# Rotary attention on one NeuronCore: which step of eight holds which small piece of work

## The chip, the cores and the metric

The kernel runs on one core of a Trainium2 chip. It is one program that computes a whole stack of eight blocks for 2048 tokens of width 256. The metric is the device time of one execution in microseconds; of the kernel before there are three timed runs and one profiled execution. Five engines work side by side: PE (TensorE, matmuls and transposes; its weight loads are listed apart as PEld), DVE (VectorE), ACT (ScalarE), POOL (GpSimd) and SP, which here only issues DMAs. Each engine takes its instructions in a fixed order and waits where one of them is not ready.

## The reference, cut to what matters

The change lies in the seventh block, an attention with rotary positions. The tokens are 32 sequences of 64 with 256 features, but the block sees each sequence as 64 channels over 256 positions; its context has the same shape. There are 8 heads of 8 channels:

```
N_HEADS, CHANNELS = 8, 64
K_CH = CHANNELS // N_HEADS
q = split_heads(_proj(x, Wq, bq))
k = split_heads(_proj(c, Wk, bk))
v = split_heads(_proj(c, Wv, bv))
q = _apply_rotary(q_emb, q)
k = _apply_rotary(k_emb, k)
scores = jnp.einsum('bhtc,bhsc->bhts', q, k) / math.sqrt(K_CH)
p_attn = jax.nn.softmax(scores, axis=-1)
out = jnp.einsum('bhts,bhsc->bhtc', p_attn, v)
out = out.transpose(0, 1, 3, 2).reshape(b, N_HEADS * K_CH, t_t)
return _proj(out, Wo, bo)
...
x = x + jnp.tanh(g_xattn[3]) * _L3_xattn_ref(_layernorm(x, axis=-1), ctx_2048, ...)
```

So each of the 32 sequences has 8 score matrices of 256 x 256, a softmax over their rows, a product with the values and an output projection.

## The kernel before, in words

The whole stack is one program. Blocks 4 and 5 run as one software pipeline; the rotary block (block6, line 1590) begins inside the end of that pipeline and then runs alone; the last block, a feed-forward with a Walsh-Hadamard transform (block7, line 1873), follows, and prepares its weights (weights7, line 1850) and its first statistics during the rotary block.

block6 is a hand-written schedule of steps, numbered g. From line 2038 on, PE, DVE, ACT and POOL keep the order in which the program names their instructions. Sequence s has two passes of four steps each:

- Steps 4s to 4s+3, the pass for the maxima. In each, `scores` (line 1675) makes a quarter of the score matrices (pp, line 1700), and DVE takes the row maxima straight from PSUM (line 1710).
- Steps 4s+6 to 4s+9, the pass for the weights. In each, `scores` makes a quarter of the transposed scores (pw, line 1686), adds the negated maxima with one more product per head (sel by top, line 1693), and ACT takes the exponential from PSUM (e, line 1706).

So from step 6 to step 127 each step first issues, for two different sequences, pw with its sel products, then pp, then the exponential and the maximum. pw and pp are 32-row matmuls that use different row strips of the array. Their PSUM tiles are a pair of banks each, taken in turn from three buffers (`pair`, line 1609), in the order pw, pp, pw, pp. A buffer is free again when ACT has taken the exponential of its pw, or DVE the maximum of its pp. So the pp of a step takes the buffer of the pw of the step before, and the pw of a step takes the buffer of the pp of two steps before.

After that each step runs the small pieces whose `due` names it (lines 1752 to 1824), in the order in which they were registered. All pieces that use PE share a pool of two PSUM banks (c.aux). They are, for sequence s, or for the pair i of sequences 2i and 2i+1:

- split (line 1662), step 4s+3: DVE, two small reductions that turn the maxima into two parts.
- shift (line 1667), step 4s+5: PE transposes the maxima twice 128 x 128 (L1671), ACT copies them to top (L1673). The sel products of step 4s+6 are the first to need them.
- mix (line 1712), steps 4s+8 and 4s+10: PE multiplies the exponentials with the values, 8 products of 128 rows by 32 columns, recorded as 16 matmuls (L1717), ACT copies the result to po_sb (L1720).
- normalise (line 1722), steps 8i+13 and 8i+15 for the two sequences: PE transposes four times (pn, L1728), DVE takes a reciprocal and a product (L1730, L1732).
- turn (line 1734), step 8i+17: two transposes (pot, L1737), ACT copies to oT (L1739).
- finish (line 1741), step 8i+23: the output projection (py, L1743), ACT adds the bias and applies the gate (y, L1745), POOL adds to x (L1746).

By the step's number modulo 8, the pieces on PE are then: 0 mix; 1 turn, then shift; 2 mix; 3 none; 4 mix; 5 normalise, then shift; 6 mix; 7 finish, then normalise.

Every 16 steps the queries of two more pairs of sequences and their keys are made (lines 1760 to 1802): in step 3 of the sixteen the query projection (`_queries`, line 402: L413 on PE, L416 on ACT, L417 on DVE), in steps 8 and 10 the queries and keys are split into two parts each (`_split_slowly`, line 464: POOL L466, then ACT L468, then POOL L470), in steps 9 and 11 DMAs on SP spread them over the partitions. These pieces are registered before the others, so in their step they come first. weights7 puts four matmuls into step 11 of some sixteens (L1859), and POOL work into later ones.

Of the kernel before, what the change touches and what calls it, by code (L numbers as in the profile page):

```python
# [1589 lines left out]
def block6(c):  # L1590
# [11 lines left out]
    with ExitStack() as es:  # L1602
# [151 lines left out]
        def due(step, what, *args):  # L1754
            steps[step].append((what, args))

        def of(what, s, *args):
            return lambda: what(seqs[s], *args)
# [47 lines left out]
        for i in range(B // 2):  # L1806
            last = i == B // 2 - 1
            for s in (2 * i, 2 * i + 1):
                due(4 * s + 3, of(split, s))
                due(4 * s + 5, of(shift, s))  # L1810
                due(4 * s + 8, of(mix, s, 0))
                due(4 * s + 10, of(mix, s, 1))
            due(8 * i + 13, of(normalise, 2 * i))
            due(8 * i + 15, of(normalise, 2 * i + 1))
            due(8 * i + 17, of(turn, 2 * i + 1))
            due(8 * i + (19 if last else 23), of(finish, 2 * i + 1))

        due(8, lambda: bias())
# [107 lines left out]
def program(tc, a, out):  # L1926
    nc = tc.nc
    with ExitStack() as es:
# [109 lines left out]
        with tc.manual_schedule(engines={mybir.EngineType.PE, mybir.EngineType.DVE, mybir.EngineType.Activation, mybir.EngineType.Pool}):  # L2038

            sixth, g, made, before6 = None, 0, 0, prologue6(c, c.first6)  # L2040
            for k, (past, done4) in enumerate(pipe):
                if past == 0 and k % 4 == 0 and made < 10 or past == 1 and k % 10 == 0:
                    next(before6, None)
                    made += 1
                if done4:
                    if sixth is None:
                        for _ in before6:
                            pass
                        k4.close()
                        keep.close()  # L2050
                        c.third = None
                        sixth = block6(c)
                        next(sixth)
                    elif k % 6 == 0:
                        next(sixth)
                        g += 1
# [131 lines left out]
```

## Time and profile before

| | us |
|---|---|
| median of three runs (lowest, highest) | 1277.58 (1267.42, 1283.98) |
| profiled execution, its own time | 1276.41 |
| its span, first to last instruction | 1274.6 |
| rotary block, steps 16 to 127 | 868.0 to 1088.6 |
| PE, DVE, ACT busy in these 220.6 us | 198.16, 174.06, 163.09 |
| mean granted TensorE clock, whole span | 0.954 |

How to read the profile: times count from the span's start. A timeline line gives the start, the duration, the engine, the line in the kernel, the operation, the tiles written and read, their shapes, how many instructions were merged, and in brackets how long the engine had been idle before and what ended that. `pw<-top,sel` is written pw, read top and sel. A line of waits gives who waited, for whom, the total time, how often and the longest. A step can be found in the timeline by the first weight load of its pw (PEld L1686), since each step begins with four of them. "issue" means that nothing the profile shows ended the wait.

### The profile page before, as it was taken

What the parts mean: (1) busy time and instruction counts of PE and PEld (TensorE: products, weight loads), DVE (VectorE), ACT (ScalarE), POOL (GpSimd) and SP (SyncE); (2) the same over time, 40 slices, a digit from 0 to 9 for tenths busy, and PEclk for the clock granted to TensorE, in tenths of its full rate; (3) what the DMA queues carried; (4) which work ended last, traced back from release to release, by engine and by line L of the source; (5) the groups of instructions that cost most, each with busy time, mean ns of one, the idle gap of its engine ahead of it and who ended that gap; (6) DMA issues with size and microseconds to landing.
All of it is one profiled execution on the core that took longest, in us unless ns stands there. A gap on an engine that the chain in (4) does not pass through costs nothing.

```text
span 1274.6 us, 21379 instructions
## 1 busy us (share of the span) xinstructions
PE 1141.2 (90%) x8086; PEld 697.0 (55%) x8086; DVE 856.8 (67%) x2133; ACT 654.0 (51%) x1131; POOL 461.7 (36%) x544
## 2 busy tenths in 40 slices
PE   3797899999999999998789998678999988999998
PEld 2575644545453337776566665335555545465565
DVE  5476858653644989877799999867878777522111
ACT  3556464331213114555789998457777767511110
POOL 3226150503012324333477777944444454000000
PEclk9988999999999999998999999759999889999999
DMA  6221010010014214000000000215334322000000
GB/s 230 96 75 66 17 42 9 1 67 1 0 74 159 67 34 170 1 1 1 2 2 2 2 2 2 67 42 182 90 94 105 98 56 53 1 14 5 16 17 17
DMA packets 26776, 62.99 MB, mean 49 GB/s; under 512 B 4144, under 2 KB 9008, under 8 KB 25520
## 3 DMA queue, kind: packets, MB, share of 16 engines
q1 hardware_dynamic: 26384, 61.60, 15.3%
q8 instruction: 64, 1.05, 0.3%
q14 instruction: 40, 0.33, 0.1%
q10 hardware_dynamic: 288, 0.00, 0.0%
HBM read 37.48 MB, written 8.39 MB: 36 GB/s over the span
## 4 chain that ended last, share of the span: by engine, by line
PE 48%; DVE 26%; POOL 8%; issue 8%; ACT 6%; DMA 2%; SPq 1%; POOLq 0%; ACTq 0%; DVEq 0%
PE pc L755 5%; PE po L1921 4%; PE pu L1911 4%; PE pg L1911 4%; PE po L1717 2%; PE pu L610 2%; PE pu L607 2%; PE pg L607 2%; PE pg L610 2%; ACT e L1706 2%; DVE xn L169 2%; PE pa L654 2%; PE po L660 1%; DVE e L1291 1%; PE pw L1686 1%
## 5 line engine op out<-in xcount | busy, mean ns | idle before, releaser
L1710 DVE TENSOR_REDUCE mx<-pp 128x4 f32<-128x1024 f32 x128 | 155.7, 1218 | 47.1 <-PE pp L1700 28.4
L1706 ACT ACTIVATE e<-pw 128x1024 f32<-128x1024 f32 x128 | 130.4, 1024 | 50.5 <-PE pp L1700 26.6
L613 ACT ACTIVATE sg<-pg 128x512 f32<-128x512 f32 (+1 forms) x75 | 37.8, 511 | 104.7 <-PE pg L607 55.9
L755 PE MATMUL pc<-xw,wb 64*64 64x512 f32 x768 | 90.0, 600 | 0.2 <-DVE x L687 0.2
L1913 ACT ACTIVATE sg<-pg 128x512 f32<-128x512 f32 x32 | 19.1, 597 | 122.8 <-PE pg L1911 122.7
L614 DVE TENSOR_TENSOR h<-pu,sg 128x512 f32<-128x512 f32 (+1 forms) x75 | 42.8, 575 | 54.5 <-PE pu L607 34.4
L1717 PE MATMUL po<-e,va 128*32 128x256 f32 x1024 | 75.1, 415 | 4.5 <-DVE t L417 2.9
L1914 DVE TENSOR_TENSOR h<-pu,sg 128x512 f32<-128x512 f32 x32 | 22.1, 691 | 80.7 <-PE pu L1911 80.4
L1700 PE MATMUL pp<-x,x 32*128 32x256 f32 x512 | 69.3, 354 | 4.3 <-ACT e L1706 4.0
L1686 PE MATMUL pw<-x,x 32*128 32x256 f32 x512 | 66.7, 344 | 2.6 <-DVE mx L1710 1.5
L1693 PE MATMUL pw<-top,sel 32*128 32x512 f32 x256 | 56.1, 441 | 10.1 <-ACT top L1673 8.4
L1686 PEld LDWEIGHTS pw<-x,x 32*128 32x128 f32 x512 | 40.4, 197 | 44.1 <-issue 26.4
L913 POOL TENSOR_TENSOR acc<-acc,sq 128x512 f32<-128x512 f32 x28 | 39.0, 1392 | 65.0 <-ACT sq L912 63.6
L1911 PE MATMUL pu<-xf,wa 128*128 128x512 f32 x128 | 60.3, 593 | 0.0
L1911 PE MATMUL pg<-xf,wa 128*128 128x512 f32 x128 | 60.3, 593 | 0.0
L755 PEld LDWEIGHTS pc<-xw,wb 64*64 64x64 f32 x768 | 30.0, 134 | 53.2 <-issue 52.5
L1921 PE MATMUL po<-hb,h 128*128 128x256 f32 x256 | 55.9, 379 | 0.0
L1921 PEld LDWEIGHTS po<-hb,h 128*128 128x128 f32 x256 | 48.8, 191 | 8.2 <-issue 1.9
L112 DVE BATCH_NORM_STATS2 ln_st<-x 128x6 f32<-128x256 f32 x112 | 44.4, 408 | 11.5 <-POOL x L1746 6.7
L1488 PE MATMUL pm<-w,xqT 128*128 128x512 bf16 x128 | 40.7, 424 | 11.0 <-DVE sh L1137 8.0
L1700 PEld LDWEIGHTS pp<-x,x 32*128 32x128 f32 x512 | 41.4, 202 | 9.3 <-ACT e L1706 6.3
L610 PE MATMUL pu<-zu,wa 128*128 128x512 f32 (+1 forms) x100 | 43.2, 526 | 3.4 <-DVE h L614 3.4
(361 smaller groups left out, 2981.8 us busy)
## 6 DMA issues: line engine op xcount, KB each, us to landing
x<-t SPq DMA_DIRECT2D x64, 128.0 KB, 2.6
x<-kt SPq DMA_DIRECT2D x56, 128.0 KB, 2.7
w<-in_l2f SPq DMA_DIRECT2D x12, 512.0 KB, 3.9
keys<-k_t SPq DMA_DIRECT2D x8, 512.0 KB, 3.4
wa<-in_l0f SPq DMA_DIRECT2D x2, 1828.0 KB, 11.5
kt<-keys SPq DMA_DIRECT2D x7, 512.0 KB, 3.5
wa<-in_l1f SPq DMA_DIRECT2D x2, 1536.0 KB, 8.6
wa<-in_l3f SPq DMA_DIRECT2D x6, 512.0 KB, 7.2
```

Source lines behind the costliest of these rows:

```text
L112: ins = c.nc.vector.bn_stats(st, c.x[:, i, :])
L607: nc.tensor.matmul(p, wt[:, k, fc], xf[:, k, :N], start=k == 0, stop=False, skip_group_check=True)
L610: nc.tensor.matmul(p, wt[:, fc], z[m, s][:, :N], start=False, stop=s == 1, skip_group_check=True)
L755: nc.tensor.matmul(pcs[h][to], w[rows, k, m, h, :], xw[rows, k, h, :, Z - m : Z - m + 32], start=m == 0, stop=m == Z)
L1686: nc.tensor.matmul(pw[:, jj, k, :], w.k[rows, h, k * P : (k + 1) * P], w.q[rows, h, :], start=k == 0, stop=False, skip_group_check=True,)
L1693: nc.tensor.matmul(pw[:, jj], sel[rows, h, :], top, start=False, stop=True, skip_group_check=True)
L1700: nc.tensor.matmul(pp[:, jj, n, :], p.q[rows, n, t * P : (t + 1) * P], p.k[rows, n, :], start=n == 0, stop=True, skip_group_check=True,)
L1706: nc.scalar.activation(e, pw, AF.Exp, scale=scale)
L1710: nc.vector.tensor_reduce(p.mx[:, t, i0 : i0 + 2, 4:6], pp, AX.X, ALU.max)
L1717: nc.tensor.matmul(po[strip(j), :], vas[a.i % 3][:, a.n, k, 2 * j + h, :], a.e[h, j][:, k, :], start=k == 0, stop=k == 1)
L1911: nc.tensor.matmul(p, wt[:, k, fc], xf[:, k, :], start=k == 0, stop=k == 1)
L1921: nc.tensor.matmul(po, h[:, f, q * P : (q + 1) * P], c.w2h[:, f, :], start=f == 0, stop=f == NH - 1)
```

## The change

The change moves small pieces between steps; no instruction is added, removed or altered.

- shift goes from step 4s+5 to step 4s+4, that is from steps 1 and 5 of eight to steps 0 and 4, where it comes behind the mix of the sequence before.
- normalise goes from 8i+13 to 8i+14 for the first sequence of a pair (step 6 of eight, behind the mix there) and from 8i+15 to 8i+18 for the second (step 2 of eight, ahead of the mix there, because it is registered earlier).
- turn goes from 8i+17 to 8i+21 (step 5 of eight). finish stays at 8i+23.
- For the last pair of sequences, the steps of the second normalise and of turn are 8i+16 and 8i+18.

By the step's number modulo 8 the pieces on PE are afterwards: 0 mix, then shift; 1 none; 2 normalise, then mix; 3 none; 4 mix, then shift; 5 turn; 6 mix, then normalise; 7 finish.

```diff
@@ -1807,12 +1807,12 @@
             last = i == B // 2 - 1
             for s in (2 * i, 2 * i + 1):
                 due(4 * s + 3, of(split, s))
-                due(4 * s + 5, of(shift, s))
                 due(4 * s + 8, of(mix, s, 0))
+                due(4 * s + 4, of(shift, s))
                 due(4 * s + 10, of(mix, s, 1))
-            due(8 * i + 13, of(normalise, 2 * i))
-            due(8 * i + 15, of(normalise, 2 * i + 1))
-            due(8 * i + 17, of(turn, 2 * i + 1))
+            due(8 * i + 14, of(normalise, 2 * i))
+            due(8 * i + (16 if last else 18), of(normalise, 2 * i + 1))
+            due(8 * i + (18 if last else 21), of(turn, 2 * i + 1))
             due(8 * i + (19 if last else 23), of(finish, 2 * i + 1))
```

## The prediction

> **What bounds the kernel now.** First the page's busy times, then the waits, then the stretch that the change touches, in order of time.
>
> ```profile
> span 1274.6 us, 21379 instructions
> PE 1141.2 (90%) x8086; PEld 697.0 (55%) x8086; DVE 856.8 (67%) x2133; ACT 654.0 (51%) x1131; POOL 461.7 (36%) x544
> ```
>
> PE is the engine to fill, but 90% is a mean. The rotary block's steps 16 to 127 run from 868.0 to 1088.6 us; there PE is busy for 198.16 of 220.60 us. The waits of this stretch (who waited, for whom; total, times, longest) say what ends PE's idle time:
>
> ```profile
> PEld pw L1693 <- ACT top L1673: 15.1, 27, 0.8
> PE pw L1693 <- ACT top L1673: 7.7, 14, 0.6
> PE pt L1671 <- ACT po_sb L1720: 5.9, 6, 2.1
> PE pp L1700 <- ACT e L1706: 3.7, 5, 0.9
> ```
>
> The first three belong to shift, which the change moves. The fourth is the one to remember: the maxima's product (pp) waits until an exponential has emptied a buffer. I then read the timeline of steps 112 to 119, which hold no other work: 14.1 us, steps beginning with the weight loads of pw at 1060.41, 1062.08, 1063.35, 1065.90, 1066.37, 1069.18, 1070.65, 1072.74 and 1074.48.
>
> ```profile
> 1062.08 0.30 PEld L1686 LDWEIGHTS pw<-x,x 32*128 32x128 f32 x4 [0.41 <-issue]
> ...
> 1063.35 0.30 PEld L1686 LDWEIGHTS pw<-x,x 32*128 32x128 f32 x4 [0.17 <-issue]
> ...
> 1064.46 0.18 PEld L1693 LDWEIGHTS pw<-top,sel 32*128 32x128 f32 x2 [0.82 <-ACT top L1673]
> ...
> 1065.90 0.30 PEld L1686 LDWEIGHTS pw<-x,x 32*128 32x128 f32 x4 [0.41 <-issue]
> ...
> 1066.37 0.31 PEld L1686 LDWEIGHTS pw<-x,x 32*128 32x128 f32 x4
> ...
> 1066.67 1.94 ACT L1706 ACTIVATE e<-pw 128x1024 f32<-128x1024 f32 x2 [0.26 <-PE pp L1700]
> ...
> 1067.75 0.30 PEld L1700 LDWEIGHTS pp<-x,x 32*128 32x128 f32 x4 [0.95 <-ACT e L1706]
> ...
> 1068.18 0.59 PEld L1717 LDWEIGHTS po<-e,va 128*32 128x32 f32 x16
> 1069.18 0.19 PEld L1686 LDWEIGHTS pw<-x,x 32*128 32x128 f32 x2 [0.41 <-issue]
> ```
>
> The step at 1065.90 has no extra work on PE, and lasts 0.47 us. The next pays for it: with three pair buffers, pp must wait for the exponential of the empty step, so the mix starts at 1068.18, **2.28 us after the empty step began** (0.77 to the exponential, 0.97 for it, 0.11 to pp, 0.43 to the mix). So a pair "odd step, next even step" never lasts less than 2.28 us plus the even step's extra work, however empty the odd one is. The pair's two products take 0.68 of an even step before its extra work (1062.08 to 1062.76 in the step with turn and shift), so an odd step hides the latency only if it lasts 2.28 - 0.68 = 1.60 us or more.
>
> In every second eight (steps 8 to 10 of 16) a query conversion sits on ACT:
>
> ```profile
> 949.39 0.62 ACT L468 CAST t<-t 128x512 fp32r<-128x512 f32 x1 [0.73 <-POOL t L466]
> 949.92 0.36 ACT L1720 COPY po_sb<-po 128x256 f32<-128x256 f32 x1
> 950.18 1.03 ACT L1706 ACTIVATE e<-pw 128x1024 f32<-128x1024 f32 x1
> 950.33 0.20 PEld L1671 LDWEIGHTS pt<-ident,mx 128*128 128x128 f32 x2 [0.99 <-ACT po_sb L1720]
> ```
>
> And the granted clock (the column before the last two) halves for a while in some such eights; the first row is an eight at full clock, the second the worst:
>
> ```profile
> 946.80:961.90 15.10, 13.63 (x165) 8.48 (x164) 12.63 (x27) 12.08 (x21) 6.09 (x6) 1.00 0.53 128
> 1006.70:1027.40 20.70, 19.35 (x165) 10.97 (x164) 13.53 (x27) 12.52 (x21) 6.07 (x6) 0.67 0.51 127
> ```
>
> **The change part by part.** Nothing is added or removed; shift (2 transposes, ACT copy to top) moves from odd steps into the mix steps 0 and 4 of eight, normalise (4 transposes, DVE reciprocal and product) into mix steps 6 and 2, turn from step 1 to 5. None of them issues a DMA or a POOL instruction, and finish with its POOL addition stays, so the queues of SP and POOL keep their order. Afterwards steps 1 and 3 are empty, 5 holds two transposes, 7 one product.
>
> Prices, by differences of steps in the timeline. The mix: 1069.18 - 1068.18 = 1.00. Shift alone on PE: pt's load at 950.33 to the next pw at 950.70, 0.37; I take 0.36. Normalise: its four loads begin at 1073.73 and the next pw at 1074.48, 0.75 later; 0.17 of that is the gap ahead of pw, which a mix step pays anyhow (its own is 0.41): 0.58. After a mix, eight transposes at 1094.05 take 1.15 to the next pw, 0.14 each, so both prices hold behind a mix too.
>
> Eight clean steps, by pairs (before from the starts above; after is 2.28 plus the even step's work):
> - 1 and 2: 3.82 (with the wait for top) becomes 2.28 + 1.00 + 0.58 = 3.86: +0.04. The wait for top goes, the wait for the exponential comes in its place.
> - 3 and 4: 3.28 becomes 2.28 + 1.00 + 0.36 = 3.64: +0.36. Step 3 was empty before too, so shift is paid in full.
> - 5 and 6: 3.56 becomes 2.28 + 1.58 = 3.86: +0.30.
> - 7 and 0: 1.74 + 1.67 = 3.41 becomes 2.28 + 1.36 = 3.64: +0.23. Step 7 loses normalise, falls from 1.74 to some 1.2 and no longer covers its exponential; step 5, with turn alone, to 1.0.
> Sum +0.93 on 14.1 us; two such eights at the end: +1.9.
>
> Sixteen steps with queries and conversions (six of them, steps 16 to 111): the pairs as above, +0.04, +0.36 (in step 3 DVE's query instructions set when the mix may start, in both kernels; shift comes on top), +0.30, then steps 7 to 10 together, +0.36, +0.30, +0.23. For 7 to 10: the cast starts 4.3 us after step 7 in both, since POOL's work before it is the same. Before, PE then waits for the copy of po and again for top: steps 7 to 10 last 1.74 + 1.67 + 2.23 + 2.53 = 8.17. Afterwards ACT does cast, copy of po, copy of top, exponential of step 9; pp of step 10 is queued on PE behind that exponential, and the mix, normalise and all later steps behind pp. Exponential from 5.4 to 6.4 after step 7, pp at 6.5, extras at 6.95, plus 1.58: 8.55, so +0.4. Sum +2.0 per sixteen, six times: +11.9.
>
> Costed at nothing: shift's wait for split, which DVE ends by 1068.4 where shift would begin at 1069.2 (behind the queries, 0.4 us early still; if late, that lateness is added to the pair). DVE's product and reciprocal, 0.54 us, only change their step; DVE is busy 11.18 of the 14.1 us of the eight. The two small PSUM buffers: in the new order (po pt, pn po, po pt, pot, po pn, py) each is taken again at least a step after its reader was issued. The first 16 steps are led by the blocks before (PE waits up to 6.2 us for their DVE there): 0, between -2 and +2. The last steps, where pp is gone: 0, between -1 and +1.
>
> Two costs have no row. Array shapes: in the new even steps 32-row, 128*32 and 128*128 matmuls follow one another. The load behind a mix waits 0.41 on "issue", behind transposes 0.17, behind pp 0.25. Least: transposes cost 0.11 each (shift in step 5: 1.47 - 1.25 = 0.22 for two): 56 even steps at -0.14 are -8. Most: 0.41 more in each: +23. I take 0, since the eight transposes behind the mix show none.
>
> The Trainium skill, TensorEngine Tiling (Array Packing), Key Properties, says that changing the tiling mode drains TensorE. By that rule it counts against the change: I count 16 switches in eight steps for 14 before, and with 0.41 for each added one 2 x 14 x 0.41 = 11.5 us would come on top.
>
> Clock: the drops at 888.6, 919.3, 1011.5 and 1049.0 us cost 1.2, 3.1, 5.6 and 1.5, 11.4 in all, by their eights against 15.1 (less 1.3 of an ACT wait in the last). Each follows steps 9 and 10, where PE idles 0.75 + 0.59 = 1.34 us. Afterwards step 10 idles about 1.35: the same, so 0. Ends: all drops gone, -11; one like the worst in each of the six, 33.6 - 11.4 = +22.
>
> The Trainium skill, TensorE: Matmul & The Clock Gate, Why this matters for your kernels, asks only for no idle gap over about 3 us; by it no drop would come at all and the sum would be 11 us lower. The trace differs: its drops follow idle pieces under 1 us.
>
> **Sum** against the profiled execution's 1276.4 (span 1274.6 and 1.8 around it): 11.9 + 1.9 = +13.8, so 1290.2. The median shown is 1277.6, 1.2 above: 1291.
>
> **The rivals.**
> - *Nothing takes the place of the waits removed* (other side): PE's idle time for top and po_sb, 7.7 + 5.9 = 13.6, is won: 1264. For it: these are the largest waits of PE here. Against: 1065.90 to 1068.18. It decides if the even step's work can begin earlier than 2.28 us after an odd step's start; the break-even is 2.28 - 0.93 / 4 = 2.05.
> - *The clock becomes the bound*: +8 to +22 on the forecast, 1299 to 1313. For it: more steps idle 0.6 us, and step 10's idle time lies closer together. Against: no clean eight shows a drop.
> - *Changes of shape cost 0.41 in each even step*: 1291 + 23 = 1314. Against: the eight transposes behind a mix.
>
> **How the numbers follow.** Forecast 0.60, own range 1282 to 1300 (shape prices at -8, the ends of the stretch at +3, and about half the 16.6 us between the runs shown); waits won 0.12; clock 0.16; shapes 0.12. Two per cent, about what a measurement of this kernel can tell from no change, is below 1252 or above 1303. Slower: half the clock case and two thirds of shapes, 0.16; faster: 0.02; same: 0.82. Leaving out about 0.08 below and 0.11 above, the range is 1270 to 1308.
>
> **What would show it.** Right: pw no longer waits for top except in step 10 of 16; pp's wait for e grows from 5 to some 50 times, about 0.6 us each; pairs of 3.86 and 3.64; a clean eight of about 15.0. Wrong: pairs under 3.5 (the latency is hidden), mix steps longer by over 0.36 and 0.58 than a bare mix (shapes), or half clock over more than 27 us of the stretch.

## The result, and the profile after

The changed kernel takes 1287.35 us (median of 17 runs, 1282.77 to 1290.75); the kernel before, over 17 runs beside them, 1273.7. The ratio is 1.0109, with a 95% interval from 1.0086 to 1.0133: slower by about 14 us, where the forecast was +13.8. The profiled execution, the slowest of the 17 runs, has a span of 1289.0 us, 14.4 more than before.

The page's first lines:

```profile
span 1289.0 us, 21362 instructions
...
PE 1152.0 (89%) x8070; PEld 694.5 (54%) x8086; DVE 859.4 (67%) x2133; ACT 655.9 (51%) x1131; POOL 462.3 (36%) x544
```

The program's instructions are the same (a few PE records are missing from the trace). PE is nevertheless busy 10.8 us longer. In the clean eight from step 112 it is busy 13.34 of 15.1 us, for 12.70 of 14.1, although its matmuls, added up one by one, take 56.5 us for 56.9: fewer of them run side by side. So a higher busy time of PE is no sign of more work here, and of the 1.0 us by which the eight grew only 0.4 show as idle time of PE. The waits of the rotary block after the change (who, for whom; total, times, longest):

```profile
PEld pp L1700 <- ACT e L1706: 25.1, 33, 1.2
...
PE pp L1700 <- ACT e L1706: 13.3, 19, 0.9
...
PEld pw L1693 <- ACT top L1673: 8.3, 6, 2.7
...
PE pw L1693 <- ACT top L1673: 7.1, 6, 2.5
```

The wait for top is left in six places only, one for each conversion, where it became longer (7.1 us in 6 waits of PE, for 7.7 in 14). pp's wait for the exponential has taken the place of the others, from 3.7 to 13.3 us. The timeline of steps 112 to 114, which begin at 1071.81, 1074.17 and 1074.42:

```profile
1072.80 0.59 PEld L1717 LDWEIGHTS po<-e,va 128*32 128x32 f32 x16
...
1073.80 0.20 PEld L1671 LDWEIGHTS pt<-ident,mx 128*128 128x128 f32 x2 [0.41 <-ACT e L1706]
...
1074.17 0.18 PEld L1686 LDWEIGHTS pw<-x,x 32*128 32x128 f32 x2 [0.17 <-issue]
...
1074.42 0.30 PEld L1686 LDWEIGHTS pw<-x,x 32*128 32x128 f32 x4
...
1074.95 1.94 ACT L1706 ACTIVATE e<-pw 128x1024 f32<-128x1024 f32 x2 [0.29 <-PE pw L1693]
...
1076.03 0.30 PEld L1700 LDWEIGHTS pp<-x,x 32*128 32x128 f32 x4 [1.13 <-ACT e L1706]
...
1076.46 0.42 PEld L1728 LDWEIGHTS pn<-ident,po_sb 128*128 128x128 f32 x4
...
1077.04 0.59 PEld L1717 LDWEIGHTS po<-e,va 128*32 128x32 f32 x16 [0.17 <-issue]
...
1078.05 0.18 PEld L1686 LDWEIGHTS pw<-x,x 32*128 32x128 f32 x2 [0.41 <-DVE rl L1730]
```

The empty step at 1074.17 is left after 0.25 us, the next one's pw is issued at once, and then PE waits: the even step's own work (pn) begins at 1076.46, 2.29 us after the empty step did. The same stretch also shows the two prices: mix to pt 1.00, pt to the next pw 0.37; pn to the mix 0.58.

| pair of steps (clean eight) | before | forecast | after |
|---|---|---|---|
| 1 and 2 | 3.83 | 3.86 | 3.87 |
| 3 and 4 | 3.28 | 3.64 | 3.65 |
| 5 and 6 | 3.56 | 3.86 | 3.87 |
| 7 and 0 | 3.40 | 3.64 | 3.65 |
| eight | 14.1 | 15.0 | 15.05 |

Where the span's 14.4 us lie, by the starts of steps: up to step 16, 865.9 for 868.0, -2.1; the six sixteens with conversions (steps 16 to 111) 205.9 for 192.4, +13.5; the two clean eights 30.11 for 28.15, +2.0; from step 128 on 187.06 for 186.03, +1.0.

### The profile page after: what moved, and what is told of

Read it like the earlier page. It is cut to its first block, busy times and chain, and to the rows that moved or that the text cites. A ratio compares the mean times of both kernels' runs of the same rounds, so it can differ in the third digit from the quotient of the medians.

```text
span 1289.0 us, 21362 instructions
## 1 busy us (share of the span) xinstructions
PE 1152.0 (89%) x8070; PEld 694.5 (54%) x8086; DVE 859.4 (67%) x2133; ACT 655.9 (51%) x1131; POOL 462.3 (36%) x544
## 4 chain that ended last, share of the span: by engine, by line
PE 53%; DVE 25%; POOL 7%; issue 6%; ACT 6%; DMA 1%; SPq 0%; POOLq 0%; ACTq 0%; DVEq 0%
PE pc L755 5%; PE po L1921 4%; PE pu L1911 4%; PE pg L1911 4%; PE po L1717 4%; ACT e L1706 2%; PE pu L610 2%; PE pu L607 2%; PE pg L607 2%; PE pg L610 2%; PE pw L1686 2%; PE pa L654 2%; DVE xn L169 2%; PE po L660 1%; PE pp L1700 1%
## 5 line engine op out<-in xcount | busy, mean ns | idle before, releaser
L1700 PE MATMUL pp<-x,x 32*128 32x256 f32 x512 | 69.3, 354 | 15.0 <-ACT e L1706 13.3
L1686 PE MATMUL pw<-x,x 32*128 32x256 f32 x512 | 63.2, 340 | 3.1 <-DVE mx L1710 1.7
L1693 PE MATMUL pw<-top,sel 32*128 32x512 f32 x256 | 51.9, 420 | 7.1 <-ACT top L1673 7.1
L1700 PEld LDWEIGHTS pp<-x,x 32*128 32x128 f32 x512 | 41.5, 202 | 29.8 <-ACT e L1706 25.1
L1746 POOL TENSOR_TENSOR x<-x,y 128x256 f32<-128x256 f32 x16 | 11.8, 735 | 109.5 <-ACT y L1745 96.4
L1488 PE MATMUL pm<-w,xqT 128*128 128x512 bf16 x112 | 38.8, 422 | 13.1 <-DVE sh L1137 7.9
```

What stands on the lines that cost most here:

```text
L1686: nc.tensor.matmul(pw[:, jj, k, :], w.k[rows, h, k * P : (k + 1) * P], w.q[rows, h, :], start=k == 0, stop=False, skip_group_check=True,)
L1693: nc.tensor.matmul(pw[:, jj], sel[rows, h, :], top, start=False, stop=True, skip_group_check=True)
L1700: nc.tensor.matmul(pp[:, jj, n, :], p.q[rows, n, t * P : (t + 1) * P], p.k[rows, n, :], start=n == 0, stop=True, skip_group_check=True,)
```

## The experiments

The theory: a pair of an odd and the next even step lasts the longer of two things, PE's work in it, or the 2.28 us from the odd step's start over its exponential and pp to the even step's extra work, plus that work. Rivals: array shapes changing in the mix steps; the waits that the change took away; the clock. All ratios are to the kernel before, run on the same chip; lengths of steps come from one profiled execution of each kernel.

**Shift alone.** Only shift goes to step 4s+4.

```diff
-                due(4 * s + 5, of(shift, s))
                 due(4 * s + 8, of(mix, s, 0))
+                due(4 * s + 4, of(shift, s))
```

> Only shift moves (to steps 0 and 4 of eight); normalise and turn stay in odd steps. Latency theory (a pair of an odd and the next even step lasts 2.28 us plus the even step's extra work, or the sum of the PE work if that is longer): pairs 1+2 3.28, 3+4 3.64, 5+6 3.28, 7+0 3.78, so a clean eight (steps 112 to 119) of 13.98 us against 14.1 before and 15.06 in the changed kernel; whole kernel within 3 us of the kernel before. Rival, changes of the array's shape in the mix steps cost the time: 28 of the 56 moved pieces stand behind a mix here too, so half of the changed kernel's loss, about +7 us, and pairs 3+4 and 7+0 longer than 3.64 and 3.78.

Measured: pairs 3.29, 3.65, 3.29 and 3.76, the eight 14.0 us: the steps are as the latency theory has them, and no half of the loss is here. The sixteen from step 48, at full clock in both, lasts 29.5 us for 29.8. The time is not as expected: 1278.59 us, ratio 1.0042 (1.0007 to 1.0077), some 5 us slower, outside the 3 us expected. In its profiled execution one eight took 20.0 us, at two thirds of the clock (third number from the end):

```profile
881.90:901.90 20.00, 18.45 (x162) 9.90 (x160) 11.62 (x17) 12.20 (x20) 6.09 (x6) 0.66 0.53 133
```

The kernel before has such an eight as well, of 20.70 us. And this execution is the fastest of the ten (1272.63 us); its steps 16 to 127 take 217.6 us, for 220.5 in the profile of the kernel before, so the loss of the median can't be read from it. The ten runs had mean clocks of 0.932 to 0.950, those of the kernel before 0.944 to 0.960. That left the clock as a suspect, which later runs test.

**Normalise and turn alone.** Shift stays in 4s+5; the other lines are as in the change.

```diff
-            due(8 * i + 13, of(normalise, 2 * i))
-            due(8 * i + 15, of(normalise, 2 * i + 1))
-            due(8 * i + 17, of(turn, 2 * i + 1))
+            due(8 * i + 14, of(normalise, 2 * i))
+            due(8 * i + (16 if last else 18), of(normalise, 2 * i + 1))
+            due(8 * i + (18 if last else 21), of(turn, 2 * i + 1))
```

> Only normalise and turn move; shift stays in steps 1 and 5. Latency theory: the wait for top stays and the odd steps get emptier: pairs 1+2 2.56 + 1.58 = 4.14, 3+4 3.28, 5+6 2.82 + 1.58 = 4.40 (turn's copy now stands ahead of top), 7+0 3.28; clean eight 15.10 us, whole kernel +14 us against the kernel before, as slow as the changed kernel with shift left where it was. Rival, shapes: +7 us. Rival, the waits for top are what matters: the whole kernel no slower than the changed one minus the waits that it keeps, that is +28 us.

Measured: pairs 4.13, 3.29, 4.42, 3.29, the eight 15.1; 1287.5 us, ratio 1.0120 (1.0061 to 1.0179), +15 us. So this half of the edit brings the whole loss, though it takes nothing out of the waits for top and puts only half of the moved pieces behind or ahead of a mix. The pairs are as expected to 0.02 us. Both the rivals' numbers (+7, +28) are missed, the lower one narrowly: the interval goes from +8 to +23 us.

**Normalise back into odd steps.** From the changed kernel:

```diff
-            due(8 * i + 14, of(normalise, 2 * i))
-            due(8 * i + (16 if last else 18), of(normalise, 2 * i + 1))
+            due(8 * i + 13, of(normalise, 2 * i))
+            due(8 * i + (16 if last else 19), of(normalise, 2 * i + 1))
```

> The changed kernel with normalise put back into odd steps, the first into step 5 (beside turn), the second into step 3; shift stays in steps 0 and 4. The same PE work as in the changed kernel. Latency theory: the odd steps stay below 1.6 us, so normalise costs nothing there: pairs 1+2 3.28, 3+4 3.64, 5+6 3.28, 7+0 3.64, clean eight 13.84 us; whole kernel 10 to 15 us faster than the changed one, that is within 4 us of the kernel before. Rival, PE's work sets the time: the eight stays at 15.06. Rival, shapes: half of the loss stays, +7 us against the kernel before.

Measured: pairs 3.29, 3.65, 3.28 and 3.66, the eight 13.9: with the same instructions as the changed kernel, 1.2 us less, so PE's work doesn't set the eight. But the whole kernel took 1286.8 us, ratio 1.0115 (1.0046 to 1.0185), about as the changed one, where I had expected it within 4 us of the kernel before. The timeline of a step 3 with queries shows what I had overlooked:

```profile
946.93 0.88 DVE L417 SCALAR_TENSOR_TENSOR t<-pr,wb,con 128x256 f32<-128x256 f32 x2 [0.24 <-ACT t L416]
947.47 0.42 PEld L1728 LDWEIGHTS pn<-ident,po_sb 128*128 128x128 f32 x4 [1.54 <-DVE t L417]
```

The queries hold both small PSUM banks, and pn waits for the first of them until DVE has read it; PE idles 1.08 us and steps 3 and 4 last 5.46 us for 3.84 before. An empty step is only free room for a piece if its buffer is free as well. Steps 11 and 12 with four matmuls of the last block's weights grew too, 2.11 + 2.03 for 1.74 + 1.66. In the sixteen from step 48, without a clock drop, all this leaves 31.0 us for 29.8, so some 7 us in six sixteens; the two profiled executions differ by 8.3 us. The rest of the median's 15 us lies within the interval, which goes from +6 to +24 us; no step shows it.

**The exponential halved, in the changed kernel and in the kernel before.** Half of the exponentials are left out; there is one execution of each.

```diff
-                e = tp.tile([P, 2, 2, D], F32, tag="e", name="e", bufs=4)
-                nc.scalar.activation(e, pw, AF.Exp, scale=scale)
+                e = tp.tile([P, 2, 2, P], F32, tag="e", name="e", bufs=4)
+                nc.scalar.activation(e, pw[:, :, :, :P], AF.Exp, scale=scale)
...
-                    nc.tensor.matmul(po[strip(j), :], ..., a.e[h, j][:, k, :], start=k == 0, stop=k == 1)
+                    nc.tensor.matmul(po[strip(j), :], ..., a.e[h, j][:, k, :].unsqueeze(1).to_broadcast([P, 2, P]), start=k == 0, stop=k == 1)
```

> The changed kernel with the exponential of half of each weight tile only (keys' columns 0 to 127 of 256; the mix reads that half twice), so half of the exponentials are left out and the PE work stays the same. Latency theory: the exponential falls from 1.02 to about 0.6 us and each latency-bound pair with it: 3.42, 3.20, 3.42, 3.33, clean eight 13.4 us against 15.06, whole kernel some 20 to 25 us shorter than the changed one. Rival, PE's work or the array's shapes set the time: the eight stays at 15.06 and the whole kernel within 3 us.

Measured: pairs 3.45, 3.23, 3.45, 3.32, the eight 13.45 us for 15.05; span 1268.9, 20.1 shorter. The same place in the timeline, for a step 113 that begins at 1057.78:

```profile
1058.56 1.09 ACT L1706 ACTIVATE e<-pw 128x512 f32<-128x512 f32 x2 [0.29 <-PE pw L1693]
1059.21 0.30 PEld L1700 LDWEIGHTS pp<-x,x 32*128 32x128 f32 x4 [0.66 <-ACT e L1706]
...
1059.64 0.42 PEld L1728 LDWEIGHTS pn<-ident,po_sb 128*128 128x128 f32 x4
```

From the step's start to pn it is 1.86 us instead of 2.29. PE does what it did before; only ACT is faster. The first three pairs are 0.42 shorter; 7+0 is only 0.33 shorter, as expected, since there PE's work becomes the longer of the two. So the exponential's latency set the time of these pairs.

> The kernel before with the exponential of half of each weight tile only, as in the run with the changed kernel: half of the exponentials are left out, PE's work stays. Latency theory: pairs 1+2 3.38, 3+4 2.84, 5+6 3.15, 7+0 3.41 (this one is bound by PE's work and keeps its length), clean eight 12.8 us against 14.1; the changed kernel's excess in a clean eight falls from 0.96 to about 0.6 us, and 7+0 alone doesn't move. Rival, PE's work: 14.1 stays.

Measured: pairs 3.41, 2.85, 3.44 and 3.38, the eight 13.1, for 12.8 expected. Pair 7+0 keeps its length (3.40), since PE's work sets it. Pair 5+6 missed: 3.44 for the 3.15 expected, still held up by top. The changed kernel's excess in an eight fell from 0.98 to 0.36 us, below the 0.6 expected, because of that pair. Span 1249.9.

**The weights' pass two steps later.** The kernel before, with top needed three steps after shift instead of one, and the odd steps as full as they were.

```diff
-                h, j0 = (g - 6) % 4 // 2, 2 * ((g - 5) % 2)
+                h, j0 = (g - 8) % 4 // 2, 2 * ((g - 5) % 2)
...
-                due(4 * s + 8, of(mix, s, 0))
-                due(4 * s + 10, of(mix, s, 1))
+                due(4 * s + 10, of(mix, s, 0))
+                due(4 * s + 12, of(mix, s, 1))
             due(8 * i + 13, of(normalise, 2 * i))
-            due(8 * i + 15, of(normalise, 2 * i + 1))
-            due(8 * i + 17, of(turn, 2 * i + 1))
-            due(8 * i + (19 if last else 23), of(finish, 2 * i + 1))
+            due(8 * i + (17 if last else 23), of(normalise, 2 * i + 1))
+            due(8 * i + (19 if last else 25), of(turn, 2 * i + 1))
+            due(8 * i + (21 if last else 31), of(finish, 2 * i + 1))
...
-            scores(at(6), at(0), g)
+            scores(at(8), at(0), g)
```

(`last` holds for the last two i here, and there are two steps more.)

> The kernel before with the weights' pass two steps later (from step 4s+8 instead of 4s+6), mix at 4s+10 and 4s+12, second normalise, turn and finish eight steps later, so that by the step's number modulo 8 the same pieces stand in the same steps, but top is needed only three steps after shift. Latency theory: the wait for top goes and the odd steps stay filled, so pairs 1+2 3.28, 3+4 3.28, 5+6 3.28, 7+0 3.41, clean eight 13.25 us against 14.1; steps 7 to 10 of a sixteen with a conversion 7.7 against 8.17; two steps more at the end, +3; whole kernel 6 to 10 us faster than before. Rival, the wait for top hides nothing but another wait: the eight stays at 14.1.

Measured: pairs 3.28, 3.29, 3.28 and 3.38, the eight 13.2; steps 7 to 10 of a conversion 7.63. The whole kernel takes 1249.2 us, ratio 0.9816 (0.9777 to 0.9856), 23 us faster: more than the 6 to 10 expected. By its stretch of 200.0 us for 220.5, 20.5 us are won there; the profiled execution has no half-clock time in it, which had cost 11.4, and the steps' part is the other 9. The timeline of steps 121 and 122 (starts at 1052.81 and 1054.07):

```profile
1053.66 0.25 PEld L1671 LDWEIGHTS pt<-ident,mx 128*128 128x128 f32 x2
...
1054.30 0.19 PEld L1693 LDWEIGHTS pw<-top,sel 32*128 32x128 f32 x2
...
1054.66 0.30 PEld L1700 LDWEIGHTS pp<-x,x 32*128 32x128 f32 x4 [0.17 <-ACT e L1706]
...
1054.76 0.39 ACT L1673 CAST top<-pt 128x256 fp32r<-128x256 f32 x1
...
1055.09 0.59 PEld L1717 LDWEIGHTS po<-e,va 128*32 128x32 f32 x16
```

sel no longer waits for the top that is copied after it, and turn and shift fill the time of the exponential: pp waits 0.17, and the mix still begins 2.28 after the odd step did.

**The conversion's addition one step earlier.** The kernel before; ACT's cast needs POOL's first addition, which stood behind finish's addition.

```diff
+            @at(g + 7)
+            def _(z):
+                z.parts = _split_slowly(nc, z.q)
+                next(z.parts)
+
             @at(g + 8)
             def _(z):
-                _split(nc, z.q)
+                for _ in z.parts:
+                    pass
```

> The kernel before with only the first POOL addition of the queries' conversion moved from step 8 to step 7 of sixteen, ahead of finish's addition, so that ACT's cast need not wait for POOL. If the PE idle time of steps 9 and 10 is what halves the clock: steps 7 to 10 last 7.5 us instead of 8.17, the pt wait for po_sb falls below 0.2 us, no or one half-clock stretch in steps 16 to 111 instead of four, and the whole kernel is 4 us faster by the wait and up to 11 us more by the clock. If the clock drops come from something else: 4 us faster, with half-clock stretches of about 27 us as before.

Measured: steps 7 to 10 last 7.34 us for 8.17, where 7.5 was expected; pt no longer waits for po_sb. 1259.84 us, ratio 0.9889 (0.9851 to 0.9927), 14 us faster. The profiled execution has no half-clock time from step 16 to 127; the eight that took 20.70 us before, at a clock of 0.67, is now

```profile
1000.60:1014.90 14.30, 13.57 (x167) 8.48 (x166) 12.67 (x27) 12.02 (x21) 4.85 (x5) 1.00 0.53 128
```

Of the 17.1 us that the stretch gained (203.4 for 220.5), six times 0.83 are steps, and 11 to 12 the clock. In six runs the mean clocks were 0.948 to 0.966, with 0.945 to 0.960 before. Whether the drops are gone from every run is not shown: there is one trace, and the mean clock covers the whole span.

**Both edits together.**

> Both edits of the two runs before: weights' pass two steps later and the conversion's addition one step earlier. Latency theory: clean eight 13.25 us, steps 7 to 10 of a conversion sixteen about 7.1 us, whole kernel 10 to 14 us faster than before by the steps, and up to 11 us more if the half-clock stretches go. If the two gains are one and the same wait: no more than the better of the two runs alone.

Measured: the eight 13.2, steps 7 to 10 6.77 for the 7.1 expected, 1249.82 us, ratio 0.9810 (0.9765 to 0.9856). The stretch is shorter than with the later weights alone (195.0 for 200.0), but the two ratios can't be told apart. Either is faster than both kernels of the study.

**Shift alone, and the changed kernel, each with the earlier addition.** The edit above on top of them.

> Shift alone moved, as in the first run, and the conversion's POOL addition one step earlier. Open is why shift alone came out about 5 us slower than before although its clean eight is 14.0 us. If that was the clock (longer half-clock stretches after steps 9 and 10): with the conversion's idle time gone this kernel is as fast as the kernel before with the same earlier addition, ratio to the kernel before between 0.985 and 0.991, no half-clock stretch in steps 16 to 111 in most runs. If shift's place costs time of its own: 5 us slower than that, ratio 0.992 or more.

Measured: ratio 0.9860 (0.9834 to 0.9885), 1257.67 us; no half-clock time in the stretch, the eight 14.0. It is no slower than the kernel before with the same edit (0.9889), so shift's new place costs nothing by itself. The 5 us of the first run are then most likely the clock's; no trace shows them, since its profiled execution was a fast one.

> The changed kernel with the conversion's POOL addition one step earlier. Latency theory: clean eight 15.06 us as in the changed kernel, steps 7 to 10 of a conversion sixteen 7.85 instead of 8.51; the excess over the kernel before with the same earlier addition stays 13 to 15 us, so the ratio to the kernel before is 0.998 to 1.002. If the clock made a good part of the change's loss: the excess falls to under 8 us, ratio 0.995 or less.

Measured: ratio 0.9978 (0.9963 to 0.9994), 1273.17 us, a little below the range expected; the eight 15.0, steps 7 to 10 7.52 for the 7.85 expected. Against the kernel before with the same edit the stretch is 217.6 for 203.4, +14.2 us. Some 1.5 us of this are one half-clock piece of 3.41 us at 1025.1, in step 2 of the sixteen from step 96. The ratios differ by 0.0089, 11 us with an uncertainty of some 5. So within this uncertainty the change costs as much with a nearly quiet clock, some 13 us by the steps.

## Why the prediction was right, point by point

- *The wait that takes the place of the one removed.* Right, pair by pair (table above), and shown by the halved exponential. The rival that nothing takes its place is out: its break-even was 2.05 us from an empty step to the next step's work; measured 2.29.
- *Where the loss comes from.* The forecast's sum had +0.04, +0.36, +0.30 and +0.23 for the pairs; measured +0.04, +0.37, +0.31, +0.25. It did not split the edit into parts. The runs did: shift early, with the odd steps left full, is neutral, as its wait and its place cancel; emptying the odd steps 1, 5 and 7 and lengthening 2 and 6 loses the 14 us.
- *Steps 7 to 10 with a conversion.* Forecast +0.4; measured 8.50 for 8.16 in the sixteen from step 48, +0.34. The order on ACT was as foreseen (cast, po, top, then the exponentials):

```profile
950.62 0.62 ACT L468 CAST t<-t 128x512 fp32r<-128x512 f32 x1 [1.17 <-POOL t L466]
...
951.40 0.38 ACT L1673 CAST top<-pt 128x256 fp32r<-128x256 f32 x1
951.67 2.07 ACT L1706 ACTIVATE e<-pw 128x1024 f32<-128x1024 f32 x2
951.83 0.18 PEld L1693 LDWEIGHTS pw<-top,sel 32*128 32x128 f32 x2 [1.35 <-ACT top L1673]
```

- *The sum.* A sixteen without a clock drop (steps 48 to 63) lasts 31.8 for 29.8, the +2.0 of the forecast; six are 12, and 13.5 were measured. The rest is where drops fell. The forecast of 1291 us stood on the median of three runs, 1277.6; over 17 runs it is 1273.7, and so the time itself came out 4 us lower, with the difference as forecast.
- *Array shapes, taken at 0 between -8 and +23.* Right: 0.37 and 0.58 behind and ahead of a mix, as in the odd steps. The Trainium skill, TensorEngine Tiling (Array Packing), Key Properties, says that changing the tiling mode drains TensorE; the gaps ahead of each load (0.17 to 0.41) agree that something is waited for, but the switches added by the change cost nothing beyond the pieces' own price.
- *The clock, taken at 0.* Nearly right in sum: 30.7 us of half clock in the stretch, for 27.3 before, though where the drops fell changed. PE's idle pieces in step 10, which the prediction put at 1.35 us as before, were 1.15 and 0.43 in the sixteen from step 48. The prediction also says that the drops follow idle pieces under 1 us; ahead of the one at 1049.0 there was one of 2.09. What I had not seen is how much these drops cost the kernel before.
- *Edges.* The first steps moved by -2.1 (bounds -2 and +2), the last by +1.0 (bounds -1 and +1): each just outside, and of opposite sign. That they and the 1.5 us of the drops nearly cancel in the span is luck.
- *Signs to look for.* pp's wait was to be seen some 50 times; it is 33 of the loads and 19 of the matmuls (0.7 us each). Of these matmuls 12 stand in step 2 of eight and 4 in step 4, as many there as before; in step 6 only loads wait, 13 times 0.4 us, and in step 0 it shows once, although these pairs grew as forecast. So the count of this wait was a poor sign. One sign of being wrong did appear, half clock over more than 27 us of the stretch (30.7); the 3.4 us more than before are worth at most 1.7 us, an estimate for the case that all work in them took twice as long. The six left-over waits for top are where they were expected.

## What to carry to other kernels

Where buffers go round in a ring, find the shortest time from one step's start over its slowest reader to the next step's work, and fill that time with small pieces; emptying a step below it buys nothing, and the pieces cost in full where they go. To remove a wait for a late operand, move its consumer later rather than the producer's neighbours about. And before placing a piece into a free step, see that its buffer is free there too.

## What the runs showed of the hardware that was not expected

Half-clock stretches of PE, in multiples of 3.4 us, follow quite short idle times. In the kernel before each of the four in the stretch began in step 10 of a sixteen with a conversion, where PE idles twice, for about 0.75 and 0.59 us within some 2.2 us in three of them, and for 2.09 and 0.59 in one. Two more sixteens with a conversion have the idle pieces of 0.75 and 0.59 and no drop (those from steps 48 and 64). Where the pieces fall in time tells them apart: the starts of the four drops lie 9, 27 and 11 times 3.41 us from one another, so they are on a grid. In the interval of this grid just ahead of each drop PE idles 1.13 to 2.39 us; in the two other conversions a grid point lies inside or between the idle pieces, and no other interval of the stretch has more than 0.93. This is no general bound: with shift alone three drops follow intervals with 0.87 or 0.88, and none follows one with 1.37. Nor are conversions the only place: one of the changed kernel's five drops, at 1036.8, came in step 2 of the sixteen from step 96, after 1.27 us of idle time.

Taking away the first of a conversion's two idle pieces with an edit on POOL was worth 14 us, of which only 5 are the wait. The Trainium skill, TensorE: Matmul & The Clock Gate, Why this matters for your kernels, warns of gaps over about 3 us; in the kernel before no single gap ahead of a drop was longer than 2.09, so the measurement decides.

The spread of a kernel's runs goes with this clock. Of the kernel before, beside the first experiments, the runs at a mean clock of 0.944 to 0.946 took 1276.6 to 1277.7 us and those at 0.959 to 0.960 took 1265.9 to 1268.5: about 0.7 us for each 0.001. Between kernels the mean says less: most of the half clock lies ahead of step 16 (88.7 us in the profile of the kernel before, 116.1 with normalise back in odd steps), and step 16 begins at about the same time all the same (868.0 and 869.7). So a comparison of a few runs within one per cent needs the clocks beside the times, and a single slow eight in a profile needs a look at its clock before its waits are read. What moves the grid against the program's steps from run to run, and what exactly an interval must hold for a drop, stays open.
